# Nine of sixteen chunks of an edge count moved from a kernel's slot stage to the last groups of its gate

## The chip, the core and the metric

The kernel runs on one core of a Trainium2 chip. The core has five engines that take their instructions in order and run beside each other: TensorE (PE, matmuls and transposes; its weight loads are listed as PEld), VectorE (DVE), ScalarE (ACT), GpSimd (POOL) and SyncE (SP, which here issues most of the DMAs). The metric is the device time of one execution in microseconds (us); the kernel before has 2103.36 us, the median of four runs (2100.11 to 2105.37).

## The reference, cut to what matters

Two layers run over 128 graphs of 64 nodes with 256 features, 8192 rows in all. Each layer is a graph block and then a feed-forward block with experts, both added to `x`. Layer 0 ends with a gate that picks one of eight experts for each row:

```python
H = gelu(layernorm(x) @ W1 + b1)                # 1024 hidden
probs = softmax(H @ Wg + bg)                    # 8 experts
assign = argmax(probs)
x = x + probs[assign] * (H @ Wd[assign] + bd[assign])
```

The feed-forward block of layer 1 routes by an attention over a million random edges (`edge_index`) between the rows:

```python
src = concatenate([edge_index[0], loops]); dst = concatenate([edge_index[1], loops])
e = leaky_relu(a_src[src] + a_dst[dst])
alpha = softmax of e over the edges with one dst
agg = segment_sum(h[src] * alpha, dst)
```

The entries of `edge_index` reach to 16384, twice the number of rows. A source past the last row is taken as the last row, an edge whose target is past it drops out. So about half of the remaining edges come from the last row, and for these the kernel only needs to know how many go to each target. That number, `cnt` (128 rows by 64 tiles), is what the change is about. It depends on `edge_index` alone and is first used in layer 1, line 1452.

## The kernel before, in words

The 8192 rows are 64 tiles of 128, in 16 groups of `GR` = 4 tiles; two groups make a part, eight parts make the whole. Code is written as generators that stop at each `yield`, and `mix` (L168) runs several of them in turn, each by its share of steps done. That fixes the order in which instructions are put on each engine; a scheduler may move some of them ahead, and `tc.issue_after(last)` orders a piece of work behind a given instruction.

**The loop over parts** (L790 to L816) runs i from 0 to 9. Three kinds of streams are mixed in it:

- `graph` (L585) is layer 0's graph block for the groups of part i, up to i = 7. Its PSUM pool `psa` has three buffers.
- `gated` (L678) is the gate for the groups of part i - 2, so for i = 8 and 9 groups 12 to 15 run with no graph block beside them. A group goes like this: four normalised tiles are transposed on PE (L699); `hidden` (L457) makes eight blocks of 128 hidden units, two fp32 matmuls each (L464) and a gelu on ACT (L467); `turned` (L705) transposes a block back (L708) and ACT copies it into `rows` (L710), four blocks behind the gelus; then come the gate's logits (L719, L723, L728) and the softmax and argmax on DVE, from `m` (L733) to `top` (L748). DVE adds up how many rows each expert has so far (`run`, L754), PE multiplies by `before` and `ones` to give each row its place within its expert (L756, L757), and DVE writes it to `pos` (L768). POOL then scatters the group's hidden rows to DRAM, sorted by expert, with eight indirect DMAs (L773, `hrows<-rows,pos`).
- `keys.collect` (L244) turns a chunk of edges into sort keys and keeps the largest of them in 96 slots a partition. It is DVE work, over a schedule of so many chunks for each i: (0, 1, 1, 2, 1, 2, 1, 2, 3, 3).

**Between the gate and the slots** (L819 to L889, called the hole below): PE sums the experts' rows (L821), DVE adds their bases (`full`, L826), and SP reads the sums into registers. Each expert's list is filled up to a whole tile with zero rows: POOL clears a tile `none` of 128 x 256 (L825), and sixteen DMAs on SP copy it to the ends of the lists (L837). Four more zero the last tiles of `yrows` (L844). DVE works out where each row's result will lie (`row_y`) and which expert and tile each slot has (`slot_e`, `slot_t`), with POOL's `iota_s` (L855) as one input.

**The slot stage** (`slots`, L913; loop at L1012). A slot is 128 sorted rows of one expert, and 68 slots always run. SP loads its hidden rows (`hin`, L939) two slots ahead, PE transposes them (`th`, L951), ACT copies them (L954), and PE multiplies by the expert's weights in sixteen fp32 matmuls (L969). DVE adds the bias (L977) and SP stores the result to `yrows` (L978). After each slot the loop draws a step of `keys.count` and, in turn, another of it or one of `keys.finish` (L320, DVE's last sort of the keys).

**The count** (L291). A key's low bits name its target row. DVE cuts these bits into two numbers, of the row within its tile and of the tile, and compares sixteen keys at a time with all 128 row numbers and all 64 tile numbers (`pairs_equal`, L201: one 128x2048 and one 128x1024 comparison a step). PE then multiplies the two one-hot matrices, one bf16 matmul of 128 x 128 by 128 x 64 a key (L311), all added up in one PSUM tile, `cnt_ps`. Sixteen chunks of 96 keys make 96 steps of 16 matmuls. At the end DVE copies the tile to `cnt` (L318).

**After the slots** a branch (L1024) runs further slots if any are needed, and layer 1 begins: POOL gathers each row's result (`back`, L1180), DVE adds it to `x` with the gate's weight (L1195) and takes statistics (L1172), and when the first part's factors are made, PE has layer 1's first transposes (L1211).

Of the kernel before, what the change touches and what calls it, by code (L numbers as in the profile page):

```python
# [2 lines left out]

# [6 lines left out]
F32 = mybir.dt.float32  # L10
# [10 lines left out]
P = 128  # L21
# [53 lines left out]
HK = 16  # L75

# [6 lines left out]
def kernel(  # L83
# [127 lines left out]
    class Keys:  # L211
# [79 lines left out]
        def count(self):  # L291

            behind = []
            for c in range(n_chunks):
                bits = self.slots.bitcast(I32)[:, c * KEPT : c * KEPT + KEPT]
                part = []
                for op, by, off in ((ALU.bitwise_and, P - 1, 0.0), (ALU.logical_shift_right, 7, -float(KEY >> 7))):
                    pi = self.work.tile([P, KEPT], I32, name="pi")
                    V.tensor_scalar(pi, bits, by, None, op)
                    pb = self.work.tile([P, KEPT], BF16, name=f"pb{by}")  # L300
                    V.tensor_scalar(pb, pi, off, None, ALU.add)
                    part.append(pb)
                for g in range(0, KEPT, HK):
                    one = []
                    for wi, pb, n in ((self.iota[0], part[0], P), (self.iota[1], part[1], NT)):
                        one.append(pairs_equal(self.twice, wi, pb[:, g : g + HK], HK, n, f"one{n}"))
                    behind.append((c * KEPT + g, one))
                    yield
                    at, one = behind.pop(0)
                    for k in range(HK):  # L310
                        nc.tensor.matmul(  # L311
                            self.ps,
                            one[0][:, k // 2, :, k % 2],
                            one[1][:, k // 2, :, k % 2],
                            start=(at + k == 0),
                            stop=(at + k == n_chunks * KEPT - 1),
                        )
            V.tensor_copy(cnt, self.ps)  # L318
# [103 lines left out]
    with tc.tile_pool(name="w0", bufs=1, reuse_waits="tile") as w0, tc.tile_pool(name="kp", bufs=1, reuse_waits="tile") as kp:  # L422
# [29 lines left out]
        with tc.tile_pool(name="bg1", bufs=1, reuse_waits="tile") as bg1, tc.tile_pool(  # L452
# [17 lines left out]
            gelus = []  # L470

            with tc.tile_pool(name="b2", bufs=1, reuse_waits="tile") as b2, tc.tile_pool(
# [3 lines left out]
            ) as psb, tc.tile_pool(name="psa", bufs=3, space=PSUM) as psa, tc.tile_pool(  # L476
                name="kc", bufs=1, reuse_waits="tile"
            ) as keys.work:
# [312 lines left out]
                for i in range(n_parts + 2):  # L791
                    next_found(i + 1)

                    def factors():
                        yield
                        make(i)
                        yield
                        if i + 2 < n_parts:
                            yield from look(i + 2, i + 1)

                    streams = []
                    if i < n_parts + 1:
                        streams.append((factors(), 6))
                    gs = range(PART * i, PART * i + PART)
                    if i < n_parts:
                        streams.append((chain(*map(graph, gs)), 15 * PART))
                    if i >= 2:
                        streams.append((chain(*(gated(g - 2 * PART) for g in gs)), 17 * PART))

                    cs = [next(chunks) for _ in range((0, 1, 1, 2, 1, 2, 1, 2, 3, 3)[i])]  # L810
                    if cs:
                        streams.append((chain(*map(keys.collect, cs)), 8 * len(cs)))
                    mix(streams)
                    if i == n_parts - 1:
                        for e in range(E0):
                            nc.sync.dma_start(wd[:, e], f0_wd[e].rearrange("(q p) f -> p q f", p=P))  # L816


            with tc.tile_pool(name="bg3", bufs=1, reuse_waits="tile") as bg3:  # L819
# [3 lines left out]

                none = bg3.tile([P, D], F32, name="none")
                nc.gpsimd.memset(none, 0.0)  # L825
# [8 lines left out]
                for e in range(E0):  # L834
                    for rows in hrows:
                        alone(
                            nc.sync.dma_start(  # L837
                                rows[bass.ds(ends[e], P), :].rearrange("p (k f) -> p k f", f=D),
                                none.unsqueeze(1).to_broadcast([P, HALF // D, D]),
                            )  # L840
                        )

                for t in range(SURE, NSLOT):
                    nc.sync.dma_start(yrows[t * P : t * P + P, :], none)  # L844
# [7 lines left out]
                for e in range(1, E0):  # L852
                    V.tensor_tensor(end[:, e : e + 1], end[:, e - 1 : e], tiles[:, e : e + 1], ALU.add)
                iota_s = bg3.tile([P, NSLOT], F32, name="iota_s")
                nc.gpsimd.iota(  # L855
                    iota_s, pattern=[[1, NSLOT]], base=0, channel_multiplier=0, allow_small_or_imprecise_dtypes=True
                )

# [31 lines left out]

        keep = ctx.enter_context(tc.tile_pool(name="keep", bufs=1, side="right", reuse_waits="tile"))
# [4 lines left out]
        if True:  # L896
            with tc.tile_pool(name="bs", bufs=3, reuse_waits="tile") as bs, tc.tile_pool(
# [9 lines left out]
                keys.psum, psl = pool("psp", 1, space=PSUM), pool("psl", 1, space=PSUM)  # L907
                keys.ps = psl.tile([P, NT], F32, name="cnt_ps")
                steps, counts = keys.finish(bm), keys.count()
# [103 lines left out]
                for t, unit in enumerate(slots(0, SURE)):  # L1013
                    with tc.issue_after(last):
                        next(counts, None)
                        next(counts if t % 2 else steps, None)
# [1159 lines left out]
```

## Time and profile before

The profiled execution took 2098.68 us itself, and its span, from the first instruction to the last, is 2097.0 us. The other runs took 2105.25, 2100.11, 2105.37 and 2101.48 us.

| stretch of the span (us) | what runs in it | PE busy | DVE busy | granted clock | DMA busy |
|---|---|---|---|---|---|
| 514.8 to 609.7 (94.9) | gate, groups 12 to 15 | 88.0 | 18.7 | 1.00 | 0.34 |
| 609.7 to 645.0 (35.3) | the hole | 2.8 | 17.5 | 0.55 | 0.60 |
| 645.0 to 991.3 (346.3) | slots | 345.7 | 278.3 | 0.99 | 0.50 |
| 991.3 to 1012.6 (21.3) | branch, first rows of layer 1 | 0.0 | 12.5 | 0.61 | 0.33 |
| 1012.6 to 2097.0 (1084.4) | layer 1 | 1031.0 | 624.4 | 0.96 | 0.44 |

Busy times are in us of the stretch; the granted clock is the share of full speed that the throttle gave TensorE; DMA is the mean busy share of the core's sixteen DMA engines. Over the whole span PE is busy 92%, DVE 64%, ACT 45% and POOL 24%. By the costliest groups of instructions, the count's 96 comparisons of 128x2048 take 116.7 us of DVE (1215 ns each) and the 96 of 128x1024 take 65.6 (683 ns each); its 1536 matmuls are down with 57.5 us of PE.

How the lines read: a timeline line gives the start, the time to the end of the last of the instructions it stands for, the engine, the line of the kernel, the operation, what is written and what is read, the shapes and how many there are; in brackets at the end stands how long the engine was idle before it and what ended that. SPq is the queue of SP. Matmuls overlap in the records (the next starts before the last has ended), so a price is read from start to start.

### The profile page before, as it was taken

How to read it: one execution, taken by the hardware profiler on the slowest of the kernel's cores; microseconds unless marked ns; L12 is line 12 of the kernel's file. 1: busy time of each engine (PE TensorE's matmuls, PEld its weight loads, DVE VectorE, ACT ScalarE, POOL GpSimd, SP SyncE). 2: the span in 40 equal slices, each digit the busy share in tenths (PEclk: the TensorE clock that was granted, in tenths of full speed). 3: DMA queues.
4: the chain of work that ended last, by engine and by line, in shares of the span. 5: the costliest groups of instructions: out<-in, count | busy, mean ns of one | idle time of the engine just before them, and what ended most of it. 6: DMA issues, size and time to landing. Idle time of an engine off the chain costs nothing. (4 is left out here: it accounts for less than half of the span.)

```text
span 2097.0 us, 32316 instructions
## 1 busy us (share of the span) xinstructions
PE 1923.8 (92%) x10422; PEld 1387.0 (66%) x10422; DVE 1340.5 (64%) x4346; ACT 941.2 (45%) x1721; POOL 494.9 (24%) x528
## 2 busy tenths in 40 slices
PE   7889989899967999999678998989999999999999
PEld 5444545444436899898356666757777767888876
DVE  6889888843126888886887656746777451333435
ACT  4867766767641222221466555323333333333422
POOL 2013122132330000000631100015555552203223
PEclk9999999999987999999778899999999999999999
DMA  8022223234226544444314211472122147988943
GB/s 241 27 94 101 91 85 112 80 132 135 112 104 220 161 158 155 161 154 121 92 54 136 65 38 42 147 204 62 51 56 66 42 154 249 296 257 275 286 128 98
DMA packets 229376, 274.96 MB, mean 131 GB/s; under 512 B 57936, under 2 KB 173520, under 8 KB 229200
## 3 DMA queue, kind: packets, MB, share of 16 engines
q1 hardware_dynamic: 194288, 212.26, 32.3%
q0 software_dynamic: 24064, 60.22, 8.8%
q8 instruction: 89, 1.46, 0.3%
q10 hardware_dynamic: 10848, 0.30, 0.3%
q14 instruction: 87, 0.71, 0.1%
HBM read 159.40 MB, written 113.22 MB: 130 GB/s over the span
## 5 line engine op out<-in xcount | busy, mean ns | idle before, releaser
L464 PE MATMUL ph<-zT,w 128*128 128x512 f32 x512 | 244.2, 601 | 5.8 <-ACT zT L700 4.4
L969 PE MATMUL py<-wd,hTt 128*128 x1088 | 246.9, 380 | 0.0
L969 PEld LDWEIGHTS py<-wd,hTt 128*128 128x128 f32 x1088 | 202.3, 191 | 24.9
L954 ACT COPY hTt<-th 128x512 f32<-128x512 f32 x136 | 73.2, 589 | 298.9 <-PE th L951 298.9
L1578 POOL DMA_INDIRECT got<-tsrc,esrc x144 | 154.9, 1076 | 206.2 <-DMA zslots<-none 84.5
L773 POOL DMA_INDIRECT hrows<-rows,pos x128 | 127.6, 997 | 301.3 <-issue 157.2
L1111 PE MATMUL py<-w,hT 128*128 128x256 f32 x800 | 188.4, 386 | 6.4 <-DVE rows L201 4.1
L1101 PE MATMUL ph<-zT,w 128*128 128x512 f32 x400 | 183.3, 599 | 0.0
L1180 POOL DMA_INDIRECT yin<-yrows,row_y x64 | 63.3, 988 | 477.7 <-SPq L1024 369.0
L1111 PEld LDWEIGHTS py<-w,hT 128*128 128x128 f32 x800 | 149.2, 191 | 36.0 <-issue 10.4
L464 PEld LDWEIGHTS ph<-zT,w 128*128 128x128 f32 x512 | 92.1, 191 | 105.2 <-issue 85.3
L2055 ACT ACTIVATE hT<-ph,b1e 128x256 f32<-128x256 f32 x152 | 71.9, 473 | 176.9 <-PE ph L2051 104.3
L1105 ACT ACTIVATE hT<-ph,b 128x512 f32<-128x512 f32 x100 | 68.6, 687 | 183.2 <-PE ph L1101 181.6
L2051 PE MATMUL ph<-zTp,w1e 128*128 128x256 f32 x608 | 139.1, 382 | 3.8 <-DMA w1e<-in_L_ffn_W_dram 3.8
L2064 PE MATMUL py<-w,hT 128*128 x608 | 137.5, 379 | 0.0
L2072 DVE TENSOR_TENSOR y<-py,b2e 128x256 f32<-128x256 f32 x76 | 32.3, 424 | 155.0 <-PE py L2064 149.7
L2051 PEld LDWEIGHTS ph<-zTp,w1e 128*128 128x128 f32 x608 | 116.6, 192 | 20.1 <-issue 4.0
L626 PE MATMUL pre<-wd 128*128 128x512 f32 x256 | 124.5, 604 | 1.8 <-ACT wd L612 1.3
L2064 PEld LDWEIGHTS py<-w,hT 128*128 128x128 f32 x608 | 112.6, 190 | 13.8
L467 ACT ACTIVATE hT<-ph,b 128x512 f32<-128x512 f32 x128 | 87.8, 686 | 74.4 <-PE ph L464 73.4
L1101 PEld LDWEIGHTS ph<-zT,w 128*128 128x128 f32 x400 | 73.0, 190 | 70.8 <-issue 69.8
L201 DVE TENSOR_TENSOR one<-iota_l,pb 128x2048 bf16<-128x2048 bf16 x96 | 116.7, 1215 | 0.2
(411 smaller groups left out, 3773.9 us busy)
## 6 DMA issues: line engine op xcount, KB each, us to landing
hin<-hrows SPq DMA_DIRECT2D x136, 256.0 KB
w1e<-in_L_ffn_W_dram SPq DMA_DIRECT2D x38, 512.0 KB
yin<-ystore SPq DMA_DIRECT2D x24, 512.0 KB
ystore<-y SPq DMA_DIRECT2D x80, 128.0 KB
zslots<-none SPq DMA_DIRECT2D x38, 256.0 KB
zin<-zslots SPq DMA_DIRECT2D x38, 256.0 KB
yslots<-y SPq DMA_DIRECT2D x76, 128.0 KB
bd<-in_L_ffn_bd_dram SPq DMA_DIRECT2D x68, 128.0 KB
```

The source lines that it names most:

```text
L201: V.tensor_tensor(o, numbers.unsqueeze(1).to_broadcast(shape), of.rearrange("p (j e) -> p j e", e=2).unsqueeze(2).to_broadcast(shape), ALU ...
L464: nc.tensor.matmul(ph, w1[:, c, q * P : q * P + P], zT[:, c, :], start=(c == 0), stop=(c == 1))
L467: gelus.append(S.activation(hT, ph, AF.Gelu, bias=b1[:, q : q + 1]).ins)
L626: nc.tensor.matmul(pre, xnT[:, c, n * P : n * P + P], wcat[:, c, :], start=(c == 0), stop=(c == 1),)
L773: nc.gpsimd.indirect_dma_start(to, bass.IndirectOffsetOnAxis(ap=pos[:, t : t + 1], axis=0), of[:, k, :], None)
L954: S.copy(hT[:, i : i + GR, :].rearrange("p q n -> p (q n)"), th)
L969: nc.tensor.matmul(py, hT[:, q, :], wd[:, bass.ds(e, 1), q, :].rearrange("p e f -> p (e f)"), start=(q == 0), stop=(q == NH - 1),)
L1101: nc.tensor.matmul(ph, w1[:, e, c, q * P : q * P + P], zT[:, c, :], start=(c == 0), stop=(c == 1))
L1111: nc.tensor.matmul(py, hTs[q][:, k * P : k * P + P], w2[:, e, q, :], start=(q == 0), stop=(q == NH1 - 1))
L1578: nc.gpsimd.indirect_dma_start(got, None, tsrc, bass.IndirectOffsetOnAxis(ap=esrc[:, b, at : at + 1], axis=0))
L2051: nc.tensor.matmul(ph, w1e[:, c, q * P : q * P + P], zT[:, c, :], start=(c == 0), stop=(c == 1))
L2064: nc.tensor.matmul(py, hTs[q][:, k * P : k * P + P], w2[:, e, q, :].rearrange("p e f -> p (e f)"), start=(q == 0), stop=(q == NH1 - 1),)
```

## The change

- **The count is split.** `count` takes a range of chunks and a number of keys a step. The first `EARLY` = 9 chunks are counted in steps of `HE` = 8 keys, 108 steps of a 128x1024 and a 128x512 comparison and 8 matmuls. The rest, 7 chunks, keep steps of 16 keys, 42 of them.
- **Where the first part runs.** When the graph block is through (i = 8), its PSUM pool `psa` and the work tiles of `collect` are closed, and the count's tiles take their place. In i = 8 and in i = 9 a stream of 43 steps is mixed with the gate's two groups. What is left, 22 steps, stands behind the tables that follow the gate.
- **Collecting** is moved ahead so that all chunks are there by then: (0, 1, 2, 2, 2, 3, 3, 3, 0, 0).
- **The slot loop** draws one step of the late count on every even slot, and steps of `finish` on the odd ones, one more on each fourth slot. What is left of either stands behind the last slot. `cnt` is the copy of the first tile and then the sum with the second.
- **Up front**: `none` and `iota_s` are made on POOL ahead of the loop over parts. `none` is 128 x 128 rather than 128 x 256, so that a zero-row DMA copies it in twice as many pieces of half the size, 512 bytes; so do the four of `yrows`.

```diff
-        def count(self):
-
-            behind = []
-            for c in range(n_chunks):
+        def count(self, cs, hk):
+
+            ps = self.pcnt.tile([P, NT], F32, name="cnt_ps")
+            first, end = cs[0] * KEPT, (cs[-1] + 1) * KEPT
+            for c in cs:
...
-                    pi = self.work.tile([P, KEPT], I32, name="pi")
-                    V.tensor_scalar(pi, bits, by, None, op)
                     pb = self.work.tile([P, KEPT], BF16, name=f"pb{by}")
-                    V.tensor_scalar(pb, pi, off, None, ALU.add)
+                    for g in range(0, KEPT, KEPT // 2):
+                        pi = self.work.tile([P, KEPT // 2], I32, name="pi")
+                        V.tensor_scalar(pi, bits[:, g : g + KEPT // 2], by, None, op)
+                        V.tensor_scalar(pb[:, g : g + KEPT // 2], pi, off, None, ALU.add)
                     part.append(pb)
-                for g in range(0, KEPT, HK):
+                for g in range(0, KEPT, hk):
                     one = []
                     for wi, pb, n in ((self.iota[0], part[0], P), (self.iota[1], part[1], NT)):
-                        one.append(pairs_equal(self.twice, wi, pb[:, g : g + HK], HK, n, f"one{n}"))
-                    behind.append((c * KEPT + g, one))
+                        one.append(pairs_equal(self.twice, wi, pb[:, g : g + hk], hk, n, f"one{n}"))
                     yield
-                    at, one = behind.pop(0)
-                    for k in range(HK):
+                    at = c * KEPT + g
+                    for k in range(hk):
                         nc.tensor.matmul(
-                            self.ps,
+                            ps,
...
-                            start=(at + k == 0),
-                            stop=(at + k == n_chunks * KEPT - 1),
+                            start=(at + k == first),
+                            stop=(at + k == end - 1),
                         )
-            V.tensor_copy(cnt, self.ps)
+            if first:
+                V.tensor_tensor(cnt, cnt, ps, ALU.add)
+            else:
+                V.tensor_copy(cnt, ps)
...
+            of_graph, of_counts = ExitStack(), ExitStack()
...
+            psa = right(of_graph, "psa", 3, space=PSUM)
+            keys.work = right(of_graph, "kc", 1, reuse_waits="tile")
+            none = bg1.tile([P, P], F32, name="none")
+            nc.gpsimd.memset(none, 0.0)
+            iota_s = bg1.tile([P, NSLOT], F32, name="iota_s")
+            nc.gpsimd.iota(
+                iota_s, pattern=[[1, NSLOT]], base=0, channel_multiplier=0, allow_small_or_imprecise_dtypes=True
+            )
...
-                    cs = [next(chunks) for _ in range((0, 1, 1, 2, 1, 2, 1, 2, 3, 3)[i])]
+                    cs = [next(chunks) for _ in range((0, 1, 2, 2, 2, 3, 3, 3, 0, 0)[i])]
                     if cs:
                         streams.append((chain(*map(keys.collect, cs)), 8 * len(cs)))
+                    if i == n_parts:
+                        of_graph.close()
+                        keys.twice = right(of_counts, "ke", 2, reuse_waits="tile")
+                        keys.work = right(of_counts, "kd", 1, reuse_waits="tile")
+                        keys.pcnt = right(of_counts, "psc", 1, space=PSUM, reuse_waits="tile")
+                        counts = keys.count(range(EARLY), HE)
+                    if i >= n_parts:
+                        n = EARLY * (KEPT // HE) * 2 // 5
+                        streams.append((islice(counts, n), n))
                     mix(streams)
...
                             nc.sync.dma_start(
-                                rows[bass.ds(ends[e], P), :].rearrange("p (k f) -> p k f", f=D),
-                                none.unsqueeze(1).to_broadcast([P, HALF // D, D]),
+                                rows[bass.ds(ends[e], P), :].rearrange("p (k f) -> p k f", f=P),
+                                none.unsqueeze(1).to_broadcast([P, HALF // P, P]),
                             )
...
                 last = V.tensor_copy(slot_t, es).ins

+            for _ in counts:
+                pass
+            of_counts.close()
+
...
-                steps, counts = keys.finish(bm), keys.count()
+                steps, counts = keys.finish(bm), keys.count(range(EARLY, n_chunks), HK)
...
                     with tc.issue_after(last):
-                        next(counts, None)
-                        next(counts if t % 2 else steps, None)
+                        next(steps if t % 2 else counts, None)
+                        if t % 4 == 1:
+                            next(steps, None)
```

## Prediction of the changed kernel's time

> **What bounds the kernel now.** First the page: its second part has PE at nine tenths and more except in slices 12 and 19, and DVE busy only up to slice 8 and again from slice 12.
>
> ```profile
> PE   7889989899967999999678998989999999999999
> DVE  6889888843126888886887656746777451333435
> ```
>
> Then the table by stage, cut at 50 us (columns: stretch, length, busy time of PE, its weight loads, DVE, ACT, POOL with counts, granted clock, DMA share, GB/s).
>
> ```profile
> 500.00:550.00 50.00, 45.43 (x196) 23.43 (x195) 14.16 (x66) 34.66 (x58) 12.04 (x12) 1.00 0.42 142
> 600.00:650.00 50.00, 16.96 (x100) 11.11 (x99) 17.52 (x87) 10.48 (x18) 11.69 (x14) 0.64 0.58 202
> 650.00:700.00 50.00, 50.00 (x447) 44.84 (x446) 39.04 (x70) 9.89 (x20) 0.00 (x0) 0.99 0.55 167
> ```
>
> Three stages touch the change: the gate's last four groups (515 to 610), where PE works 45 of 50 us and DVE is nearly free; a hole of 35 us; and the slot stage (645 to 991), where PE never rests. The hole, from the timeline of 600 to 662:
>
> ```profile
> 608.62 1.06 PE L728 MATMUL ms<-sel,hT 128*128 128x8 f32 x8
> 615.32 0.17 DVE L768 CAST pos<-m 128x4 int32<-128x4 f32 x1
> 615.40 0.16 DVE L826 TENSOR_TENSOR full<-ms,base 128x8 int32<-128x8 f32 x1
> ...
> 626.11 0.31 POOL L825 MEMSET none<- 128x256 f32 x1
> 626.45 11.77 SPq L837 DMA_DIRECT2D hrows<-none  x16
> 631.07 0.20 DVE L889 CAST slot_t<-es 128x72 int32<-128x72 f32 x1
> 642.30 3.03 SPq L939 DMA_DIRECT2D hin<-hrows  x6
> 645.02 1.94 PE L951 MATMUL th<-ident,hin 128*128 128x128 f32 x8 [9.96 <-DMA hin<-hrows]
> ```
>
> The last line's bracket: PE waits for the first slot's rows. What holds them is SP: its sixteen zero-row DMAs wait for a memset that stands behind eight scatters on POOL, and the row loads stand behind them. The slot stage's price of the count comes from PE's timeline there:
>
> ```profile
> 662.79 0.64 PE L311 MATMUL cnt_ps<-one,one 128*128 128x64 bf16 x16
> 667.63 1.13 PE L311 MATMUL cnt_ps<-one,one 128*128 128x64 bf16 x32
> 672.96 0.65 PE L311 MATMUL cnt_ps<-one,one 128*128 128x64 bf16 x16
> 978.95 1.07 PE L951 MATMUL th<-ident,hin 128*128 128x128 f32 x8
> 983.31 1.04 PE L951 MATMUL th<-ident,hin 128*128 128x128 f32 x8
> ```
>
> A slot with 16 count matmuls lasts 4.84 us (662.79 to 667.63), with 32 it lasts 5.33, with none 4.36 (978.95 to 983.31). So 16 cost 0.484 us, 30 ns each, nothing on top.
>
> **Slot stage: minus 30.5.** 95 blocks of 16 stand there now (96 less the one ahead of the first transposes). The built order of the changed kernel has 32 between the slots: 63 x 0.484 = 30.5 us less, since PE is the bound. DVE loses work there too, and DMA stays at half. Safe to 2 us.
>
> **Gate's last groups: plus 21.8.** The built order puts 632 of the 864 early matmuls (79 steps of 8) between the first transposes of group 12 (514.8) and the logits of group 15 (609.7). PE's price: 632 x 0.030 = 19.1. A bf16 matmul between two gelu passes also shows the next weight load: around L757 two passes take 0.97 us (542.82 to 543.79) against 0.86, which is 0.11, of it 0.03 the matmul; 45 blocks stand so, 45 x 0.08 = 3.6 (bounds 0 and 0.15 a block, so 0 to 6.8). PE's own gaps:
>
> ```profile
> 537.91 0.74 PE L708 MATMUL tz<-ident,hT 128*128 128x128 f32 x5
> 538.89 0.66 PE L708 MATMUL tz<-ident,hT 128*128 128x128 f32 x4 [0.24 <-ACT rows L710]
> 540.90 1.14 PE L699 MATMUL tz<-ident,z 128*128 128x128 f32 x8 [1.36 <-ACT rows L710]
> 542.20 0.18 PE L756 MATMUL ms<-top,before 128*128 128x32 bf16 x1 [0.16 <-DVE top L748]
> ```
>
> At 0.108 a transpose that is 0.44 + 1.58 + 0.31 and a tenth, 2.4 a group, 9.7 in four, all of which the counts can fill. But the softmax now shares DVE with compares. A 128x2048 compare follows the next instruction by 1.13 us and a 128x1024 one by 0.60 (654.16, 655.29, 655.89), so 128x512, which has no row, is taken on their line at 0.335 (bounds 0.30, half of 0.60, and 0.60, a floor). A step of 8 keys is 0.60 + 0.335 and 0.12 for cutting the keys up. In the built order 12 compares stand among the nine links from m to top (5.6 + 0.9 + 0.3 = 6.8 us), and m itself stands behind compares that need a buffer which PE frees only after the logits: 1.3 more. PE has 6.8 us of work before L756 (20 transposes 2.2, three gelu matmuls 2.6, 56 counts 1.7, edges 0.3): 1.3 late. The running sum L754, with three compares between, takes 2.0 against 1.1 of work: 0.9 late. So 2.2 us of new waits a group, 8.8 in four (bounds 0 and 4). Sum: 19.1 + 3.6 - 9.7 + 8.8 = 21.8, a period of some 28.8 for 23.3. DVE has 25 us of work in it and doesn't set it.
>
> **The hole: plus 5.1.** From the last logits (609.7) to the first slot transposes (645.0) is 35.3 now. After, on DVE: 1.3 as above; to pos 17 compares (8.0), 17 links (1.8), key cutting (0.8) and a wait of 0.3, so 12.2; then 16 compares and their keys (8.8) stand before L826, which ends at 21.0, not 5.9. SP needs 0.95 from it to its first DMA (615.56 to 616.5 on the queue, where it then sat until 626.45 for the memset, a wait that goes). The zero rows start at 22.0, though the memset is early: 16.8 before, so later by 5. They write 512 pieces of 512 B instead of 256 of 1024 B. The trace's packets take 26 ns for 512 B (L286) and 46 for 1024, on 16 engines 0.83 us a DMA instead of 0.74 (bounds 0.74, if pieces cost nothing, and 1.28, if the queue's 0.55 of issue grows with them): 13.3, ending at 35.3. Landing 2.4 and, as now, 2.7 from the row loads to PE: 40.4. The other path, DVE's compares up to the count matmuls that stand before L951 on PE, ends at 39. So 40.4 - 35.3 = 5.1, with bounds 3 and 12. Iota_s made early saves DVE its 7.9 us wait at L872, which is then covered by that path. The four zero DMAs of yrows (2.2 on SP) stand near 35 us, behind the loads, where the table shows DMA at 0.09: nothing. The chunks' collection ends beside the same group in both orders: nothing, give or take 2.
>
> The Trainium skill ("DMA: Bandwidth & Descriptors", Specifications) asks for at least 512 B a transfer for line rate. By it the smaller pieces would be free and this term 3.6; the rows differ by 13%, and the measurement is used.
>
> **The end of the slots: plus 6.9.** Of 42 late steps the slot loop draws 34, every second slot. In the built order 14 compares (7 steps) are left on DVE behind the last slot's add, 11 behind the branch, and the next stage's first add stands behind them.
>
> ```profile
> 991.29 0.42 DVE L977 TENSOR_TENSOR y<-py,bd 128x256 f32<-128x256 f32 x1 [3.03 <-PE py L969]
> 999.47 0.48 DVE L1195 SCALAR_TENSOR_TENSOR x<-yin,psel,x 128x256 f32<-128x256 f32 x1 [5.38 <-DMA yin<-yrows,row_y]
> ```
>
> From 991.7: 7 x 1.73 + 1.2 of keys + 0.8 branch + 1.4 memsets + 0.5 for PE's last counts = 16.0 against 7.8, so 8.2 late. Six of the first eight gathered rows then lie ready, two wait for a freed buffer, so 1.3 is caught up: 6.9. PE starts on it (1012.63, clock 0.5) and DVE is 43 of 50 busy after, so I carry it whole (bounds 3 and 8.5).
>
> **Sum.** 21.8 + 5.1 - 30.5 + 6.9 = +3.3 on the profiled execution, 2098.7 (span 2097.0): 2102.0. That execution lies 4.7 under the median of 2103.36, so the time given is 2106.7. A measurement here can tell 0.2%, 4.2 us: between 2099.2 and 2107.6 counts as the same. The forecast's own range is 2101 to 2112.
>
> **Rivals.** *Faster: the counts slip into PE's gaps.* No new waits (-8.8), the hole at its lower bound (-2.1), the stage change at 5 (-1.9): -9.5, so 2094. For it: DVE is busy 14 of 50 us there, and PE waits 2.4 a group. Against it: the compares stand between the links of the very chain that PE waits for.
>
> *Slower: the scatter sets the groups' period.* The next group's first copy into rows needs the last group's four scatters landed. The waits of 460 to 630 show ACT at rows for that DMA 1.9 us in two places already, with pos 5.5 after the logits. After, pos comes at 12.2; then 1.0 to POOL, 3.8 to the fourth scatter, 2.9 to landing: 19.9. From that copy to the next logits is 10.7 of today's PE time and 1.9 of counts, less some 3.6 by which PE can run ahead on two buffers: 28.9, level with the 28.8 above. It decides from there on. The second scatter took 1.51 at 520.02, beside a 128x1024 DVE add, instead of 0.96; with all so, 1.7 more, and without the run-ahead 3.6 more: up to 11 us in three rounds, 2117. Against it: the gelu passes give ACT slack of 0.5 a pass.
>
> The Trainium skill ("SBUF — State Buffer", "Who interferes with whom") says that a DVE instruction with two SBUF inputs contends with a GpSimd instruction that reads SBUF. The compares have two; by it every scatter beside them would pay as the one at 520.02 did, by the rest of the rows only that one.
>
> *A rival by size:* compares of 512 at 0.60 make a DVE period of 30 and add 11 in all, 2118. *That the change doesn't do what it says* is out: the built order shows the counts beside groups 12 to 15, 29 steps behind them.
>
> **Chances.** Forecast 0.42 (0.03 faster, 0.18 same, 0.21 slower by its own range), faster rival 0.26 (0.24, 0.02, 0), slower rivals 0.32 (0, 0.03, 0.29): 0.27, 0.23, 0.50. The range takes both rivals in and the bounds of the hole: 2091 to 2121.
>
> **What would show it.** Slots at 4.36 and 4.84 in turn; a group period near 28.8, with PE idle ahead of L756 and L757; the zero rows starting some 22 us after the last logits; the first L1195 some 16 after the last L977. I am wrong if the period is under 27 (compares cheaper, or the chain not slowed), over 30.5 with ACT waiting for hrows, or if the 11 late compares run ahead of the branch.

## The result and the profile after

The changed kernel takes 2104.43 us (median of 36 runs, 2100.07 to 2107.92) against 2102.63 of the kernel before (58 runs): a ratio of 1.0006, with an interval from 1.0000 to 1.0012. A second set of runs beside each other gave 1.0020 (1.0011 to 1.0029). So the change costs some 2 to 4 us, at the edge of what can be told from nothing. Inside, though, the stages moved by up to 32 us, against each other.

This table is the core of what follows; the second profiles are those of the runs `before_again` and `after_again`. Each column is a stretch of the span of one profile, in us: up to the logits of group 11; from there to the last logits of group 15; the hole, from there to the first slot transposes; the slots, to the start of the last L977 (L1002 after); from there to the first add of layer 1 (L1195, L1221 after); the rest.

| profile | to group 11 | groups 12 to 15 | hole | slots | end | layer 1 | span |
|---|---|---|---|---|---|---|---|
| before | 510.4 | 99.3 | 35.3 | 346.3 | 8.2 | 1097.5 | 2097.0 |
| before, second profile | 513.4 | 99.3 | 35.3 | 347.0 | 8.1 | 1097.6 | 2100.7 |
| after | 505.4 | 120.7 | 45.0 | 314.0 | 17.2 | 1098.9 | 2101.1 |
| after, second profile | 507.8 | 119.8 | 45.1 | 314.7 | 17.3 | 1098.0 | 2102.6 |

After against before, first profiles: -5.0 + 21.4 + 9.7 - 32.3 + 9.0 + 1.4 = +4.2 (4.1 unrounded). The page of the changed kernel shows it in its second part (slices of 52.5 us). DVE, at 1 and 2 tenths in slices 11 and 12 before, is at 8 there; PE's hole has moved from slices 12 and 13 (6 and 7 tenths) into the 13th alone, at 4:

```profile
PE   7889889998994999998678998989999999999999
DVE  6889989934887777535887656746777451334435
```

**The groups.** First a whole group before, then one after, from the tables by stage (stretch, length, busy time of PE, its weight loads, DVE, ACT, POOL, clock, DMA share, GB/s):

```profile
560.90:584.70 23.80, 22.04 (x99) 11.56 (x98) 3.27 (x18) 15.76 (x27) 7.68 (x8) 1.00 0.23 89
```

```profile
537.30:566.04 28.74, 28.02 (x268) 17.02 (x267) 24.34 (x76) 15.96 (x27) 8.96 (x8) 1.00 0.20 74
```

PE is busy for all but 0.7 us of that group; DVE has gone from 3.3 to 24.3 us. From logits to logits the four groups after take 31.9, 28.8, 29.4 and 29.6 us; before, they took 26.6 and three times 23.9. PE's waits in the four groups (engine, line, releaser, us, times, longest) hold no L774 and no L775, the changed kernel's lines for L756 and L757; the two longest are

```profile
PE cnt_ps L315 <- DVE one L204: 2.3, 3, 1.4
PE tz L717 <- ACT rows L728: 2.2, 3, 1.2
```

**The hole**, from the timeline of 624 to 675, and then its row of SP's queue:

```profile
625.01 1.06 PE L746 MATMUL ms<-sel,hT 128*128 128x8 f32 x8
638.31 0.16 DVE L786 CAST pos<-m 128x4 int32<-128x4 f32 x1
639.23 5.11 POOL L791 DMA_INDIRECT hrows<-rows,pos  x1 [17.23 <-issue]
647.66 0.16 DVE L850 TENSOR_TENSOR full<-ms,base 128x8 int32<-128x8 f32 x1
```

```profile
648.79 16.75 SPq L861 DMA_DIRECT2D hrows<-none  x16
668.27 3.11 SPq L964 DMA_DIRECT2D hin<-hrows  x6
```

The zero rows no longer wait for POOL. They wait for `full`, 21.6 us behind the last logits (626.07) where it came 5.7 behind them, and they take 16.75 us instead of 11.77.

**The slots.** From PE's timeline: a slot without a count lasts 4.33 us (697.74 to 702.07), one with 16 count matmuls behind it 4.85 (702.07 to 706.92), and they take turns:

```profile
697.74 3.62 PE L994 MATMUL py<-wd,hTt 128*128 x16
702.07 3.62 PE L994 MATMUL py<-wd,hTt 128*128 x16
706.92 3.62 PE L994 MATMUL py<-wd,hTt 128*128 x16
```

**The end**, on DVE: seven late steps' compares stand between the last slot's add and the first add of layer 1.

```profile
985.01 0.43 DVE L1002 TENSOR_TENSOR y<-py,bd 128x256 f32<-128x256 f32 x1 [1.71 <-PE py L994]
999.41 0.69 DVE L204 TENSOR_TENSOR one<-iota_h,pb 128x1024 bf16<-128x1024 bf16 x1
1002.21 0.47 DVE L1221 SCALAR_TENSOR_TENSOR x<-yin,psel,x 128x256 f32<-128x256 f32 x1
```

### The profile page after: what moved, and what is told of

It is laid out like the page before. It is cut to its first block, busy times and chain, and to the rows that moved or that the text cites. A ratio compares the mean times of both kernels' runs of the same rounds, so it can differ in the third digit from the quotient of the medians.

```text
span 2101.1 us, 32593 instructions
## 1 busy us (share of the span) xinstructions
PE 1937.2 (92%) x10422; PEld 1399.6 (67%) x10422; DVE 1362.8 (65%) x4519; ACT 941.2 (45%) x1721; POOL 505.2 (24%) x528
## 5 line engine op out<-in xcount | busy, mean ns | idle before, releaser
L471 PE MATMUL ph<-zT,w 128*128 128x512 f32 x512 | 254.4, 611 | 5.7 <-ACT zT L718 4.2
L791 POOL DMA_INDIRECT hrows<-rows,pos x128 | 136.6, 1067 | 320.5 <-issue 183.8
L1127 PE MATMUL ph<-zT,w 128*128 128x512 f32 x400 | 183.3, 599 | 0.0
L204 DVE TENSOR_TENSOR one<-iota_l,pb 128x1024 bf16<-128x1024 bf16 (+1 forms) x150 | 125.2, 835 | 19.9 <-PE cnt_ps L315 19.3
L2098 DVE TENSOR_TENSOR y<-py,b2e 128x256 f32<-128x256 f32 x76 | 32.3, 424 | 154.7 <-PE py L2090 151.9
```

Source lines behind the costliest of these rows:

```text
L204: V.tensor_tensor(o, numbers.unsqueeze(1).to_broadcast(shape), of.rearrange("p (j e) -> p j e", e=2).unsqueeze(2).to_broadcast(shape), ALU ...
L471: nc.tensor.matmul(ph, w1[:, c, q * P : q * P + P], zT[:, c, :], start=(c == 0), stop=(c == 1))
L791: nc.gpsimd.indirect_dma_start(to, bass.IndirectOffsetOnAxis(ap=pos[:, t : t + 1], axis=0), of[:, k, :], None)
L1127: nc.tensor.matmul(ph, w1[:, e, c, q * P : q * P + P], zT[:, c, :], start=(c == 0), stop=(c == 1))
```

## The experiments

The theory at this point: PE is the bound in the slots and in the gate's groups alike, so the count's matmuls cost there what they cost before, and everything else (hole, end) is lost to compares that stand ahead of something on DVE. The chief rival: the compares in the softmax chain set the groups' period, not PE.

In two of the three series (the eight runs from `zero_first` to `few_compares`) layer 1 took 12 to 23 us longer than in the table, and the kernel before, run beside them, had medians of 2119.2 and 2120.6 us. So whole times are compared within a series, and stages only where they agree across series.

### What the early count costs the groups

`few_matmuls`, one early matmul in eight:

```diff
                     for k in range(hk):
+                        if hk == HE and k and at + k != end - 1:
+                            continue
                         nc.tensor.matmul(
```

> The changed kernel with only one of each eight early count matmuls (the other seven are left out, so the count is wrong); every compare stays. Theory A (PE is the bound in the gate's last groups, each matmul costs its 0.030 to 0.034 us there): 553 of the 632 beside the groups are gone, so from group 11's logits to group 15's 120.7 us become 101 to 106, and a group's period 24 to 26 instead of 29. Rival B (the compares between the softmax's links, or the wait for their buffers, set the period): 116 to 121, PE idle for the rest.

`few_compares`, two keys a step:

```diff
+                    some = 2 if hk == HE else hk
...
-                        one.append(pairs_equal(self.twice, wi, pb[:, g : g + hk], hk, n, f"one{n}"))
+                        one.append(pairs_equal(self.twice, wi, pb[:, g : g + some], some, n, f"one{n}"))
...
-                            one[0][:, k // 2, :, k % 2],
-                            one[1][:, k // 2, :, k % 2],
+                            one[0][:, k % some // 2, :, k % 2],
+                            one[1][:, k % some // 2, :, k % 2],
```

> The changed kernel with all early matmuls, but compares of only two keys a step (128x256 and 128x128) whose result all eight matmuls read (so the count is wrong). Theory A (PE is the bound): from group 11's logits to group 15's 116 to 120 us for 120.7, since only PE's 6 us of idle time can go, and the hole gets shorter, 36 to 40 for 45, as the links and the sums wait for short compares. Rival B (DVE's compares set the period): 100 to 110.

`few_both`, the two edits together:

> The changed kernel with one of each eight early matmuls and with compares of two keys a step (few_matmuls and few_compares together; the count is wrong). Without the matmuls alone the four groups took 118.1 us, without the compares alone 125.7. Theory A (PE and DVE are bounds of nearly the same height, so that neither edit alone shows much): with both the groups return to 102 to 107, the kernel before's 99 to 102 and a little for what is left. Rival B (something else that the count brings along, its buffers or the scatters beside it, sets the period): 113 or more.

The four groups' rows of the tables by stage, for few_matmuls, few_compares and few_both:

```profile
508.20:626.30 118.10, 105.93 (x488) 53.81 (x487) 96.36 (x306) 66.04 (x106) 33.85 (x32) 0.96 0.30 107
```

```profile
507.40:633.10 125.70, 114.65 (x1039) 71.05 (x1037) 53.19 (x306) 66.02 (x106) 30.80 (x32) 0.99 0.28 102
```

```profile
505.90:612.20 106.30, 100.04 (x488) 55.07 (x487) 52.27 (x306) 66.28 (x106) 30.86 (x32) 0.97 0.33 119
```

In the series of the first two the four groups, with the count whole, take 126.6 (in `drain_behind`, below). Without seven eighths of the matmuls they take 8.4 less, where theory A wanted 15 to 20: it is missed, and the time falls to rival B. But the matmuls themselves cost PE what theory A says. From start to start, waits left out, the count's take 5.1 us for 21.9 in `drain_behind`, 16.8 less. About 7 us of that come back because PE's other matmuls and transposes take longer, at a granted clock of 0.96 for 1.00, and 1.2 because PE is idle longer (12.2 us for 10.9). And PE waits only 2.7 us for compares there. It waits 6.2 for `rows` on ACT, 3.1 of it in one piece:

```profile
PE tz L728 <- ACT rows L730: 6.2, 3, 3.1
PE cnt_ps L317 <- DVE one L204: 2.7, 5, 0.8
```

and ACT, by its own waits, stands 11.0 us ahead of `rows` for the scatters of the group before to land:

```profile
ACT rows L730 <- DMA hrows<-rows,pos: 11.0, 3, 4.5
```

So what lies under PE's bound is neither compares nor their buffers as such but the loop through the softmax, the scatters and `rows`, which the prediction had as its slower rival: the compares make `pos` late, that makes the scatters late. What it costs shows in part as clock: right behind waits of 1.87 and 3.13 us for `rows` (at 586.61 and 616.74) the granted clock is 0.63 to 0.80 for some 6 us each time. A third such stretch, at 514, follows a wait of 1.24 that the changed kernel has too without a drop, so not all of the 7 us is the loop's. With the compares short and the matmuls whole, ACT's waits hold no scatter, and the time is 0.9 less: theory A for the groups. (For the hole it is missed, 44.3: the sums come 24.2 after the logits, and DVE's compares wait 6.1 us for PE's matmuls on the way.)

Both edits together are worth 13.5 against the changed kernel beside them (119.8), and 106.3 stands in the range given: PE's count matmuls take 15.8 us less (5.6 for 21.4), ACT waits 3.0 us for scatters where it waited 11.0 in few_matmuls, and the gelu matmuls take what they take in the changed kernel. So each edit alone shows 8.4 and 0.9, and both show 13.5, because long compares without matmuls open waits, and with them and a lower clock half of the gain is lost. How long the loop would be at full clock no run shows. What the two edits leave, 7.0 us over the 99.3 of before, is 5.6 for the count matmuls left and 3.1 for longer gelu matmuls beside them, less 1.8 of idle time.

The whole follows: few_both has a ratio of 0.9891 (0.9874 to 0.9908), few_matmuls 0.9980 (0.9962 to 0.9998), few_compares 1.0055 (1.0040 to 1.0071).

### The hole

`zero_first`, before with an early zero tile:

```diff
+            none = bg1.tile([P, P], F32, name="none")
+            nc.gpsimd.memset(none, 0.0)
+            iota_s = bg1.tile([P, NSLOT], F32, name="iota_s")
...
-                none = bg3.tile([P, D], F32, name="none")
-                nc.gpsimd.memset(none, 0.0)
...
-                                rows[bass.ds(ends[e], P), :].rearrange("p (k f) -> p k f", f=D),
-                                none.unsqueeze(1).to_broadcast([P, HALF // D, D]),
+                                rows[bass.ds(ends[e], P), :].rearrange("p (k f) -> p k f", f=P),
+                                none.unsqueeze(1).to_broadcast([P, HALF // P, P]),
```

> The kernel before, with the zero tile (128x128, so pieces of 512 B) and the slot numbers made ahead of the loop over parts, and nothing else. Theory A (the early zero tile is worth its wait, and in the changed kernel the compares ahead of the expert sums ate it): the zero rows start about 1 us after the sums, 6.8 us after the last logits where they started 16.8 after them. Their sixteen DMAs take between 11.8 (as in the kernel before) and 16.8 us (as in the changed kernel), and 2.7 + 2.8 us go from their end to the first slot transposes: a hole of 24 to 29 us for 35.3, so 6 to 11 us less in the whole, 2092 to 2097. Rival B (the zero rows then share the DMA engines with the last scatters, whose end sets the row loads): the hole stays within 2 us of 35.3 and so does the whole.

`zero_by_dve`, with pieces as before:

```diff
-                nc.gpsimd.memset(none, 0.0)
+                V.memset(none, 0.0)
```

> The kernel before, where DVE instead of POOL clears the zero tile (128x256, so the pieces stay at 1024 B) and the slot numbers are made up front. In the run zero_first the zero rows started 6.8 us after the last logits, but their sixteen DMAs, in pieces of 512 B and beside the last scatters, took 19.6 us instead of 11.8, and the hole was 31.7 for 35.3. Theory A (the smaller pieces made them slow): with 1024 B they take 12 to 13, and the hole is 25 to 27, 9 to 10 us less than before. Rival B (they share the DMA engines with the last eight scatters, 4 MB and 2 MB): they take 17 to 20 whatever the pieces, and the hole is 31 to 34, 1 to 4 us less than before.

SP's queue in zero_first, then in zero_by_dve:

```profile
622.17 19.57 SPq L841 DMA_DIRECT2D hrows<-none  x16
```

```profile
622.10 16.93 SPq L841 DMA_DIRECT2D hrows<-none  x16
```

Both start the zero rows 9 to 10 us sooner, and the hole is 31.7 and 31.1 for 35.3. Theory A of zero_first (24 to 29) is missed and so is its rival (within 2); of the two for zero_by_dve, rival B holds: 16.9 with the pieces of before, so most of the loss is the company of the scatters. The zero rows are 4.2 MB and the eight scatters 2.1, and the DMA view of the hole says how fast they go (GB/s in 40 slices, of 610 to 646 before, and of 640 to 672 after):

```profile
GB/s 0 0 0 0 0 0 0 0 141 150 291 214 141 228 287 141 155 291 209 150 339 341 343 347 344 345 341 347 347 338 341 345 346 345 340 26 5 205 380 273
```

```profile
GB/s 0 0 0 0 20 0 323 123 210 282 46 236 203 300 314 277 294 350 277 363 276 359 284 289 282 286 289 294 288 287 288 287 284 290 198 0 74 302 320 335
```

Alone, the zero rows in pieces of 1024 B run at 343 GB/s; in pieces of 512 B, which also come from a zero tile half as wide, at 287. In zero_first the DMA engines are busy for eight tenths and more while the zero rows run (busy tenths in 40 slices, of 615 to 648):

```profile
DMA  0000000000899999899999899999999999810999
```

So the early zero tile is worth about 4 us of the hole, not 10: started sooner, the DMAs only overlap the scatters on engines that are full. The whole times don't show even that: zero_first has a ratio of 1.0012 (0.9987 to 1.0036), zero_by_dve 0.9981 (0.9961 to 1.0001). Against each other the pieces cost 2.6 us beside the scatters (19.57 and 16.93), though only 0.6 of it reaches the hole, since zero_by_dve keeps three of the last tiles' four zero DMAs ahead of the row loads.

In the changed kernel the hole's 9.7 us are then 6.0 for a later start (22.7 for 16.8, by `full`) and 5.0 for longer DMAs (16.75 for 11.77), less 1.3 for the four zero DMAs of the last tiles, which are out of the way. `drain_behind` takes the wait for `full` away:

```diff
-            for _ in counts:
-                pass
+            with tc.issue_after(last):
+                for _ in counts:
+                    pass
```

> The changed kernel, with the count steps that are left after the gate put behind the slot tables on DVE instead of among the softmax, the sums and the tables. Theory A (the compares ahead of the sums make the hole longer): the sums 9 to 10 us after the last logits instead of 21.6, the zero rows at 10 to 11; PE's transposes now stand behind the remaining 20 steps, whose compares DVE begins some 18 after the logits and does at 0.94 a step: 37 to 40 for the hole instead of 45.0, the whole 5 to 8 less than the changed kernel. Rival B (the hole is set by the zero rows' DMAs beside the scatters): 30 to 34. Rival C (the compares have to be done before the slots wherever they stand): 44 to 46, no difference.

The sums come 9.2 us after the logits, the zero rows' first DMA 10.4, and the sixteen take 19.6; the hole is 36.3, between theory A's 37 to 40 and rival B's 30 to 34. Theory A had the wrong thing last: it is SP's queue, as in zero_first, while the compares are still under way. They then stand in the first slots: the slots take 320.2 for 314.0, so 6.2 of the 8.7 us gained are given back. The whole, 1.0026 (1.0004 to 1.0049), has no run of the changed kernel beside it and says no more than that.

### The end, and less counted early

`late_drawn`:

```diff
                         next(steps if t % 2 else counts, None)
+                        if t % 4 == 3:
+                            next(counts, None)
```

> The changed kernel, where the slot loop draws a late count step on three slots of four instead of two, so that none is left behind the last slot. Theory A (the 11 compares left behind the branch delay the first rows of layer 1): from the last slot's add to the first add of layer 1 17.2 us become 8 to 9, the slots get 8 more blocks of 16 matmuls, 3.9 us, so 4.5 to 5.5 less than the changed kernel, which puts it level with before or 1 us under. Rival B (the gathers of the first rows, not DVE, set that stretch, or layer 1 makes the time good later): the whole at the changed kernel's time plus 0 to 4.

`early_seven`, late_drawn and

```diff
-EARLY = 9
+EARLY = 7
...
-                        n = EARLY * (KEPT // HE) * 2 // 5
+                        n = EARLY * (KEPT // HE) // 2
```

> As late_drawn, but with 7 chunks counted early instead of 9, so that all of the early count lies beside the gate's groups and none behind them: DVE has the experts' sums right after the last group's positions. Theory A (the hole grew because the sums stand behind compares): from the last logits to the first slot transposes 45.0 us become 33 to 36 (the sums some 8 after the logits instead of 21.6, then 1 to the zero rows, 13 to 17 for them, 5.5 to the transposes, and the count's first block of late steps in PE's way costs nothing), the slots get 12 more blocks than late_drawn, 5.8 us: 3 to 6 less than late_drawn, 2095 to 2098. Rival B (the zero rows' small pieces beside the scatters set the hole): 40 or more, and the whole no better than late_drawn.

In late_drawn the end is 8.2 for 17.2 and the slots 318.4 for 314.0: theory A by stage, 4.6 us less. The first add of layer 1 follows the last slot's add as it did before:

```profile
997.74 0.43 DVE L1002 TENSOR_TENSOR y<-py,bd 128x256 f32<-128x256 f32 x1 [3.03 <-PE py L994]
1005.92 0.48 DVE L1223 SCALAR_TENSOR_TENSOR x<-yin,psel,x 128x256 f32<-128x256 f32 x1 [5.32 <-DMA yin<-yrows,row_y]
```

The whole doesn't show it: 1.0042 (1.0022 to 1.0063), where theory A wanted level with before. Its four groups took 125.1 and not 120.7 in this series, with the same code there; whether that is the series' slower transfers was not settled. In the two series with the longer layer 1 the four groups take 125.1 to 126.6 us with the whole early count and 99.3 to 102.2 without any, so there it costs 23 to 27 and not 21; PE is idle for 10.2 and 10.9 us in late_drawn and drain_behind, for 6.3 in the first profile after. In early_seven the sums stand right behind `pos`, 8.5 us after the logits, and the hole is 34.7 (theory A: 33 to 36); the slots take 322.3. It is 0.9995 (0.9971 to 1.0019), 10 us under late_drawn in the same series, where 3 to 6 were expected.

### The chunks' collection

`collect_early`:

```diff
-                    cs = [next(chunks) for _ in range((0, 1, 1, 2, 1, 2, 1, 2, 3, 3)[i])]
+                    cs = [next(chunks) for _ in range((0, 1, 2, 2, 2, 3, 3, 3, 0, 0)[i])]
```

> The kernel before, with only the schedule of the chunks' collection moved ahead, (0,1,2,2,2,3,3,3,0,0). Theory A (the 5.0 us by which the changed kernel reaches the logits of group 11 sooner, 505.4 against 510.4, come from the new order of DVE's work in the first parts, 4 of them around group 1, where PE waits 2.2 us instead of 3.5 for a row sum on DVE): group 11's logits at 505 to 506, the whole 4 to 6 less, 2097 to 2099. Rival B (they come from the pools' new places or from one execution to the next): group 11's logits at 509 to 511, the whole within 2 us of before.

Group 11's logits come at 508.2, between theory A's 505 to 506 and rival B's 509 to 511; zero_first, on the old schedule in the same series, has them at 513.1. The whole is at 0.9963 (0.9943 to 0.9982), 7.8 us less: clear of rival B's 2, with an interval (4 to 12) that holds theory A's 4 to 6. So it is theory A, though its 505 to 506 was missed. Four profiles of kernels with the old schedule reach that point at 510.4 to 513.4, ten with the new one at 505.4 to 510.1. Of the 5 us between the two kernels 2.4 to 3.5 are lost between the logits of group 0 and group 1 (43.1 and 43.4 us before, 39.6 and 41.0 after), where PE waits for a row sum on DVE ahead of the gate's sixteen logit matmuls; before (second profile) and after:

```profile
144.43 3.64 PE L719 MATMUL ms<-hT,wg 128*32 128x512 f32 x16 [3.51 <-DVE deg L563]
```

```profile
142.68 1.92 PE L737 MATMUL ms<-hT,wg 128*32 128x512 f32 x16 [2.18 <-DVE deg L581]
```

The line collect_early has there reads 3.53 us after a wait of 2.44. The wait is 3.5 us in all four profiles on the old schedule and 2.0 to 2.4 on the new. After the long one the sixteen matmuls take 2.8 to 3.6 us instead of 1.92; after the short one they do so in five profiles of ten. Where the rest of the 5 us is lost was not followed.

### The two kernels again, and one without an early count

> The kernel before, unchanged, for its stages on the chip of this series (layer 1's first groups and the gate's last take some us longer here than in the first profiles). Theory A (the stages differ between the two kernels as the first profiles say): group 11's logits at 511 to 513, from there to group 15's 99 to 102 us, the hole 35 to 36, the slots 346, from the last slot's add to the first add of layer 1 8. Rival B (the 5 us up to group 11 were one execution's chance): group 11's logits at 506 to 509.

> The changed kernel, unchanged, on the same chip as before_again. Theory A: group 11's logits at 506 to 510, to group 15's 121 to 126 us (22 to 24 more than before_again), the hole 43 to 46, the slots 314, the end 17: stage by stage -4, +23, +9, -32, +9, so 4 to 7 us over before. Rival B (on this chip, with its slower transfers, the longer hole and the groups' scatters weigh more): 10 or more over before.

Their rows are in the first table. The stages are those of the first profiles to within 1.1 us, but for the point where group 11 is reached (513.4 and 507.8: the 5 us stand). The groups' 119.8 lie under the 121 to 126 expected. The time came at +3.7 against before_again and +3.2 against all runs of before in the series, just under theory A's 4 to 7; rival B is out.

`without_early`, the kernel before with collect_early's and zero_by_dve's edits and

```diff
-                    nc.sync.dma_start(yrows[t * P : t * P + P, :], none)
+                    nc.scalar.dma_start(yrows[t * P : t * P + P, :], none)
...
                 more = weights()
+                for _ in range(6):
+                    with tc.issue_after(last):
+                        next(counts)
```

> No early count: the kernel before with the chunks collected on the new schedule, the slot numbers made up front, the zero tile cleared by DVE (pieces of 1024 B), the four zero DMAs of the last tiles on ACT's queue, and five of the count's 96 steps in the hole behind the slot tables, where it had one. Theory A (the gains of the change's small parts stand without the moved count, and the count is free only where PE idles): 4 less up to group 11, the hole 28 to 31 instead of 35.3 (4 for the earlier zero rows, 1 to 2 for the four DMAs), the slots 1.9 less: 9 to 12 us under before, a ratio of 0.994 to 0.996. Rival B (the parts get in each other's way: the compares or the earlier transfers hold the first slots): within 4 of before.

2088.6 us, 0.9947 (0.9932 to 0.9961): 13 under before, better than either kernel, a little over theory A's 9 to 12. By stage against before_again: -7.7 up to group 11, 0.0 in the groups, -5.3 in the hole, -3.7 in the slots, +0.5 at the end. The profile is of the fastest of its six runs, and layer 1 is 1.7 shorter in it. Of the 3.7 in the slots 1.9 were expected, for four blocks fewer; the rest was not followed. The five count steps fit in front of the first slot's transposes in PE's empty time:

```profile
622.38 1.87 PE L311 MATMUL cnt_ps<-one,one 128*128 128x64 bf16 x32 [12.01 <-DVE one L201]
634.98 1.08 PE L951 MATMUL th<-ident,hin 128*128 128x128 f32 x4 [3.91 <-DMA hin<-hrows]
```

## Why the prediction was right, and where its steps were wrong

The time (2106.7 forecast, 2104.4 measured) and the sum on the profiled execution (+3.3 forecast, +4.1 found) are right. Their four terms are right in sign, and in mechanism but for the gaps in the groups; three are off by 2 to 5 us, and one of 5 us was missed. That the misses nearly cancel, so that the sum is off by 1 us, is luck. By the forecast's own measure the time lies among the same (2099.2 to 2107.6), to which it gave 0.23; slower had 0.50.

- **Slots, -30.5: -32.3.** PE is the bound, and a slot with one block takes 4.84 us as before. An empty slot takes 4.33, 0.03 less than the 4.36 read from one of before, which over 34 slots is one of the 1.8 us between.
- **Groups, +21.8: +21.4 and +20.5.** The size is right, and of its terms PE's own. From start to start, waits left out, 632 matmuls take 21.3 us of PE (0.031 each within a block, 0.055 on the mean for the last of one) where I had 19.1, and the gelu passes 3.1 more, where I had 3.6. The gaps are where the working failed: I let the counts fill 9.7 us and the softmax open 8.8 new ones, 2.2 a group ahead of L756 and L757. PE waits there not at all. Its idle time went from 8.1 to 6.3, and the waits left are for count tiles and for `rows`. So a net of -0.9 was right within 1 us for a reason that was not there, and that is luck. The period of 28.8 was worked out from 23.3 before; the trace has 23.9 (536.99, 560.87, 584.75), and three of the four periods after are 28.8 to 29.6.
- **Hole, +5.1: +9.7**, inside the bounds of 3 and 12. `pos` came 12.2 after the logits (12.2 forecast), `full` 21.6 (21.0), the first zero row 22.7 (22.0). The mis-sized term is the sixteen DMAs, 13.3 against 16.75: I had priced the smaller pieces from single packets (0.83 us a DMA), and left out that the first of them now run beside the last scatters; before, the last scatter was issued at 625.11 and the zero rows began at 626.45. At 287 GB/s their 4.2 MB are 14.6 us, an estimate; by it some 1.3 of the 3.5 is the pieces, and the rest the company of the scatters. The rest, 1.1, is a start 0.7 later and 5.5 instead of 5.1 from the last DMA to PE.
- **The Trainium skill** ("DMA: Bandwidth & Descriptors", "Specifications") puts line rate at 512 B and more. Here pieces of 512 B run at 287 GB/s and pieces of 1024 B at 343, so the measurement differs, by a sixth.
- **End, +6.9: +9.0 at the first add, +9.4 at PE's first transposes.** From the end of the last add to the first one of layer 1 I had 16.0 us; 16.8 came. I took 1.3 off because gathered rows lay ready; nothing was caught up. late_drawn shows the cause: without the compares it is 8.2 again.
- **Collection, "nothing, give or take 2": -5.0.** I looked for where collecting ends, not for what DVE's new order does to PE in the parts before. collect_early shows the term alone.
- **The faster rival** (no new waits) was half right on the waits and is out by the hole and the end. **The slower rival**, the scatter loop: ACT waits for the scatters' landing ahead of `rows` 9.9 us in four groups instead of 1.9, but PE only 2.9 for `rows`; it was near and did not decide. It was priced level with PE (28.9 and 28.8 a group). few_matmuls shows that it comes next: without most of the matmuls PE waits for `rows`, and half of their price is lost again.
- **The page** was read too smoothly: PE is under nine tenths in twelve slices, with its 6s in slices 12 and 20, not in two. Nothing was worked out from that.
- The 32 scatters beside the compares take 36.6 us of POOL for 31.2, and 30.8 in few_compares. The Trainium skill ("SBUF — State Buffer", "Who interferes with whom") states that a DVE instruction with two SBUF inputs contends with a GpSimd instruction that reads SBUF. The longer scatters agree with it, but few scatters pay much: six of the 32 took over 1.3 us, 19 under 1.1. One scatter behind the groups, at 639.23 with compares back to back, took 5.11 instead of 0.96.

## What to carry to other kernels

Work moved from one stage that an engine bounds to another that the same engine bounds is worth nothing, however empty the other engines look there; move it to where that engine is idle (five steps of sixteen keys in the hole didn't lengthen it, seventy-nine of eight beside the gate cost 21 us). When the moved work has two halves, price each engine's path alone: if the two come out near each other, taking one away opens waits on the other, a lower clock behind them can give half of the gain back, and only an experiment with both tells what the whole costs. Before counting a wait as removed, look at what the released transfers will then run beside: ten us of earlier start were worth four in their stage.

## What the runs showed of the hardware

- Zero rows in pieces of 512 B wrote 287 GB/s, in pieces of 1024 B 343; with eight scatters beside them sixteen such DMAs of 256 KB took 19.6 and 16.9 us, alone 11.8 (1024 B).
- In group 1, over fourteen profiles, PE's sixteen logit matmuls took 1.92 us after each of five waits of 2.02 to 2.31 us, and 2.81 to 3.64 after each of nine of 2.34 to 3.52; in the kernel before, where the wait is 3.51, the granted clock is 0.50 from 144 to 148 us.
- The first indirect DMA of group 15 took 5.10 or 5.11 us on POOL, in all four profiles in which compares of 128x1024 and 128x512 run back to back on DVE beside it, and 0.96 in the kernel before.
